# A four-layer graph stack on one core: own row and row pairs of the layer-2 heads added on GpSimd, output weights held stationary, and the row weighting of layers 1 and 3 put on GpSimd

## The chip, the core and the metric

The kernel runs on one core of a Trainium2 chip. The metric is device time in microseconds (us) of one execution, the median of a few runs. Matmuls run on TensorE (PE in the profile, its weight loads PEld), elementwise work on VectorE (DVE), ScalarE (ACT) and GpSimd (POOL); SP only starts DMAs. Everything here is float32.

## The reference

Eight batches of 2048 nodes with 64 features pass through four layers. Each layer normalizes its input, applies relu, attends over the neighbours that a sparse 0/1 matrix `adj` names, and adds the result to its input:

```python
# layer 0: softmax over neighbours of h h^T / 8, times h
# layer 1: h = x W; e = leaky(s1[n] + s2[m]); softmax over neighbours; times h; elu
# layer 2: four heads h_k = x Wh_k; per head softmax over neighbours and self of h_k h_k^T, times h_k
z   = leaky_relu(concat(heads))            # 256 features
h2  = z @ Wo.T                             # 64 features
out = layernorm(leaky_relu(softmax(h2 h2^T over neighbours and self) @ h2 + bo)) * gamma + beta
# layer 3: as layer 1, with relu at the end
for each layer: x = x + layer(relu(layernorm(x)), adj)
```

## The kernel before

The 2048 nodes are 16 **row blocks** of 128 nodes (partitions); a row holds all 8 batches, 512 numbers. Neighbours are not multiplied through a dense matrix: a setup stage turns `adj` into lists, and each block gets a number of **row slots**, 84 in all. A slot is one indirect DMA on GpSimd's queue (`gather`, L227) that brings one row for each of 128 partitions into a ring of 30 slots. The first `ROWS[i]` slots of a block hold the first neighbours of the block's own nodes, so partition p belongs to node p. The other `PACKED[i]` slots hold the remaining neighbours of all its nodes packed together; a 0/1 matrix `sel` (and its transpose `selt`) tells which node each belongs to. Per block, in the order of work:

- order of blocks: 15, 14, 13, 0, 12, 11, 10, 1, 9, 2, 8, 3, 7, 4, 6, 5
- slots of each: 3, 3, 3, 17, 3, 4, 4, 8, 4, 7, 4, 6, 4, 5, 4, 5
- of these own-node slots (`ROWS`): 2, 1, 1, 7, 1, 3, 3, 5, 3, 5, 3, 5, 2, 3, 1, 4

Every layer runs as a **pipeline** over the blocks: in step n, the last stage works on an old block and the first on a new one, and stages are issued from the last to the first. Within that program order the compiler's scheduler orders each engine's instructions by its own estimates; each engine then takes its own list strictly in order.

**Weighted sums** of layers 0, 1, 3 and of layer 2's output attention are made in `weigh_sum` (L316 to L333). For each pair of slots an elementwise engine multiplies the two gathered rows with the softmax weights (L326, a tile `wg`), and TensorE adds them up in PSUM (L331): with the identity matrix as the stationary operand for own-node slots, with `selt` for packed ones. The multiplication runs on GpSimd, except in layers 1 and 3. There `first` (L464 to L485) has ScalarE copy the weights into a small PSUM tile (`tiny`, L484), and `check` passes this copy and VectorE to `weigh_sum`.

**Layer 2's heads** are stages `take2, turn, first2, second2, third2, fourth2` (L655 to L762). `first2` forms, for head pair k = 0 and 1 in turn, the queries of the block (L685, L690), spreads them to the packed slots (L697) and has VectorE multiply and reduce query times row (`dot`, L669 and L673: one pair of instructions for the own row and each slot), then exponentials on ScalarE (L381). `second2` makes the weighted sums, for each head pair: two PSUM tiles `ys`; the block's own row, weight 1, is added with two identity matmuls (L721); then for each slot GpSimd forms `wg`, 128x1024 (L724), and two matmuls add it to `ys` (L727). VectorE divides (`yn`, L731). `third2` transposes `yn` (L741), applies the head weights (L745), bias and leaky relu. `fourth2` applies the output weights `wo_sb`: 32 small matmuls of 64 columns for each block, each with another 128x128 tile of `zt` as the stationary operand (L756), a ScalarE copy (L759), and a store to a table in memory that the next stage gathers from.

Some further lines: L255 (`ln_r`, a power on GpSimd, part of each normalization), L304 (a running sum of rows on GpSimd). The file also has a dense fallback that runs only if a list overflows; it doesn't run here.

Of the kernel before, what the change touches and what calls it, by code (L numbers as in the profile page):

```python
# [8 lines left out]
F32 = mybir.dt.float32  # L9
# [4 lines left out]
OP = mybir.AluOpType  # L14
AX = mybir.AxisListType

P = 128
# [9 lines left out]
ROWS = [7, 5, 5, 5, 3, 4, 1, 2, 3, 3, 3, 3, 1, 1, 1, 2]  # L27
# [22 lines left out]
def edge_stack(ctx: ExitStack, tc: tile.TileContext, x_in, adj, w1, w1t, a1, wh, wht, bh, wo, bo,  # L50
# [9 lines left out]
    nc = tc.nc  # L60
    N, F = x_in.shape
    D = gamma.shape[0]
    B = F // D
# [10 lines left out]
    work = ctx.enter_context(tc.tile_pool(name="work", bufs=2))  # L74

    ident = const.tile([P, P], F32, name="ident")
# [51 lines left out]
    with tc.tile_pool(name="setup", bufs=1) as sp, \  # L128
# [24 lines left out]
        for h in range(H):  # L153
            p = ps_w.tile([P, D], F32, name="p")
            nc.tensor.matmul(p, wh2[:, h].rearrange("d t c -> d (t c)"), wh2[:, h, 0, :],
                             start=True, stop=True)
# [11 lines left out]
    wo_sb = const.tile([P, 2, D], F32, name="wo")  # L168
# [33 lines left out]
    def tiny(n):  # L202

        at = spot[0] if spot[0] + n <= F else 0
        spot[0] = at + n
        return bank[0][:, at:at + n]
# [106 lines left out]
    def lhs(i, t):  # L313

        return ident if t < ROWS[i] else selt(i, t - ROWS[i])

    def weigh_sum(i, st, w, own=None, eng=nc.gpsimd):

        y = ps_y.tile([P, F], F32, name="y")
        g, n = st["g"], SLOTS[i]  # L320
        if own is not None:
            nc.tensor.matmul(y, ident, own, start=True, stop=False)
        for t0 in range(0, n, 2):
            m = min(2, n - t0)
            wg = work.tile([P, 2, F], F32, name="wg")
            eng.tensor_tensor(  # L326
                wg[:, :m].rearrange("p t (b d) -> p t b d", b=B),
                g[:, t0:t0 + m, :F].rearrange("p t (b d) -> p t b d", b=B),
                w[:, t0:t0 + m, :, None].to_broadcast([P, m, B, D]), op=OP.mult)
            for t in range(t0, t0 + m):  # L330
                nc.tensor.matmul(y, lhs(i, t), wg[:, t - t0, :], start=(t == 0 and own is None),  # L331
                                 stop=(t == n - 1))
        return y  # L333
# [63 lines left out]
        w = slots(w_all, i)  # L397
        exps(i, w, scores(i, st, st["rows"]), mba, D ** -0.5)

    def second(i, st, wp=None):  # L400
        w = slots(w_all, i)
        d, p = by_query(i, w, B)
        st["rec"] = small.tile([P, B], F32, name="rec")
        nc.vector.tensor_tensor(st["rec"], p, d, op=OP.add)
        nc.vector.reciprocal(st["rec"], st["rec"])
        st["y"] = weigh_sum(i, st, w) if wp is None else weigh_sum(i, st, wp, eng=nc.vector)
        done(i, st)

    def divide(st, dst):
# [35 lines left out]
    def additive(k, wd, *finish):  # L445
        def take(i, st):
            gather(k, i, st)

        def sums(i, st):
            w = slots(w_all, i)  # L450
            nc.scalar.activation(w, st["g"][:, :, F:], AF.Exp, scale=1.0 / TEMP)
            d, p = by_query(i, w, B)
            S = small.tile([P, B], F32, name="S")
            nc.vector.tensor_tensor(S, p, d, op=OP.add)
            nc.vector.tensor_reduce(most[:, 1, i:i + 1], S, AX.X, OP.max)
            nc.vector.tensor_reduce(least[:, 1, i:i + 1], S, AX.X, OP.min)
            lg = tiny(B)
            nc.scalar.activation(lg, S, AF.Ln)
            st["fs"] = small.tile([P, 2, B], F32, name="fs")
            z = small.tile([P, B], F32, name="z")  # L460
            nc.vector.scalar_tensor_tensor(z, lg, TEMP, f1s[:, i, :], op0=OP.mult, op1=OP.add)
            nc.scalar.copy(st["fs"][:, 0, :], f1s[:, i, :])
            leaky(st["fs"][:, 1, :], z)

        def first(i, st):
            K, T, g = ROWS[i], PACKED[i], st["g"]
            w = slots(w_all, i)
            s = slots(s_all, i)
            fs = st["fs"].rearrange("p t b -> p (t b)") if k == 4 else f1s[:, i, :]
            n = 2 * B if k == 4 else B  # L470
            pr = tiny(2 * B)
            nc.scalar.copy(pr[:, :n], fs)
            pv = by_edge(i, fs, n)
            nc.vector.tensor_tensor(s[:, :K, :], g[:, :K, F:], pr[:, None, :B].to_broadcast([P, K, B]), op=OP.add)
            nc.vector.tensor_tensor(s[:, K:, :], g[:, K:, F:], pv[:, :, :B], op=OP.add)
            leaky(s, s)
            if k == 4:
                nc.vector.tensor_tensor(s[:, :K, :], s[:, :K, :], pr[:, None, B:].to_broadcast([P, K, B]),
                                        op=OP.subtract)
                nc.vector.tensor_tensor(s[:, K:, :], s[:, K:, :], pv[:, :, B:], op=OP.subtract)  # L480
                nc.vector.tensor_scalar(s, s, 60.0, None, op0=OP.min)
            nc.scalar.activation(w, s, AF.Exp)  # L482
            wp = tiny((K + T) * B)
            nc.scalar.copy(wp, w.rearrange("p t b -> p (t b)"))  # L484
            st["wp"] = wp.rearrange("p (t b) -> p t b", b=B)  # L485

        def check(i, st):
            second(i, st, st["wp"])
            if k == 1:
                nc.vector.tensor_reduce(most[:, 0, i:i + 1], st["rec"], AX.X, OP.max)  # L490
                nc.vector.tensor_reduce(least[:, 0, i:i + 1], st["rec"], AX.X, OP.min)

        def third(i, st):
            st["att"] = work.tile([P, F], F32, name="att")
            divide(st, st["att"])
            st["xt"] = transposed(st["att"])

        def project(i, st):
            p = st["p"] = ps_q.tile([P, F], F32, name="q")
            for j in range(F // P):  # L500
                nc.tensor.matmul(p[:, j * P:(j + 1) * P], st["xt"][:, j, :], wd, start=True, stop=True)
            finish[0](i, st)

        mid = [sums] if k == 4 else []
        pipeline(take, *mid, first, both(check, xs_rows), third, project, *finish[1:])
# [145 lines left out]
    with tc.tile_pool(name="l2", bufs=2) as l2p, \  # L651
# [54 lines left out]
        def second2(i, st):  # L706
            g, n = st["g"], SLOTS[i]
            w = st["w"]
            d, p = by_query(i, w.rearrange("p t b h -> p t (b h)"), B * H)
            rec = st["rec"] = small.tile([P, B, H], F32, name="rec2")  # L710
            rf = rec.rearrange("p b h -> p (b h)")
            nc.vector.scalar_tensor_tensor(rf, p, 1.0, d, op0=OP.add, op1=OP.add)
            nc.vector.tensor_reduce(most[:, 2, i:i + 1], rf, AX.X, OP.max)
            nc.vector.reciprocal(rf, rf)
            st["yn"] = []
            for k in range(2):
                hs = slice(2 * k, 2 * k + 2)
                ys = [ps_y.tile([P, 4, 2, D], F32, name="y") for _ in range(2)]
                xb = heads(st["rows"])[:, :, None, :].to_broadcast([P, B, 2, D])
                for j in range(2):  # L720
                    nc.tensor.matmul(ys[j], ident, xb[:, 4 * j:4 * j + 4], start=True, stop=False)  # L721
                for t in range(n):
                    wg = work.tile([P, B, 2, D], F32, name="wg")
                    nc.gpsimd.tensor_tensor(wg, heads(g[:, t, :F])[:, :, None, :].to_broadcast([P, B, 2, D]),  # L724
                                            w[:, t, :, hs, None].to_broadcast([P, B, 2, D]), op=OP.mult)
                    for j in range(2):
                        nc.tensor.matmul(ys[j], lhs(i, t), wg[:, 4 * j:4 * j + 4], start=False,  # L727
                                         stop=(t == n - 1))
                for j in range(2):
                    yn = l2p.tile([P, 4, 2, D], F32, name="yn", bufs=4)  # L730
                    nc.vector.tensor_tensor(yn, ys[j], rec[:, 4 * j:4 * j + 4, hs, None].to_broadcast([P, 4, 2, D]),  # L731
                                            op=OP.mult)
                    st["yn"].append(yn.rearrange("p b h d -> p (b h d)"))
            done(i, st)
# [15 lines left out]
                st["zt"].append(zt)  # L750

        def fourth2(i, st):
            p = ps_m.tile([P, F], F32, name="m")
            for b in range(B):
                for k in range(2):
                    nc.tensor.matmul(p[:, b * D:(b + 1) * D], st["zt"][2 * k + b // 4][:, b % 4, :],  # L756
                                     wo_sb[:, k, :], start=(k == 0), stop=(k == 1))
            h2 = work.tile([P, F + B], F32, name="xh", bufs=3)
            nc.scalar.copy(h2[:, :F], p)  # L759
            store_rows(3, i, h2, False)  # L760

        pipeline(take2, turn, first2, second2, third2, fourth2)  # L762
# [1 line left out]
    with psum_pools()[0] as ps_q, psum_pools()[1] as ps_t, tc.tile_pool(name="rows2", bufs=2) as rp:  # L764
# [66 lines left out]
        p = ps_m.tile([P, F], F32, name="m")  # L831
# [516 lines left out]
```

## Time and profile before

| | us |
|---|---|
| median of 3 runs | 2215.48 (2214.14 to 2217.83) |
| the profiled execution: its time | 2214.14 |
| its span, first to last instruction | 2212.4 |
| busy PE / DVE / POOL / ACT | 1535.5 / 1404.1 / 1108.3 / 615.7 |
| mean granted TensorE clock | 0.821 |

The stages follow one another in the trace, with the gathers of a stage waiting for the table that the stage before stored:

| stage | window, us | PE busy | DVE busy | POOL busy |
|---|---|---|---|---|
| layer 1 | 475 to 710 | 152.5 | 126.4 | 109.6 |
| layer 2, heads | 710 to 1624 | 756.5 | 558.7 | 397.0 |
| layer 3 | 1985 to 2212 | 155.4 | 100.1 | 80.3 |

In a group line, the name left of the arrow is the tile written, the ones right of it the tiles read; then shapes, the number of instructions, busy us, mean ns of one, and the idle time just before. A float32 matmul stands in the trace as two MATMUL records, so 672 records of L727 are 336 matmuls. Matmuls are pipelined, so their mean is longer than their share of busy time. "issue" in a chain or wait is time in which the profile shows no releaser.

### The profile page before, as it was taken

How to read it: one execution, taken by the hardware profiler on the slowest of the kernel's cores; microseconds unless marked ns; L12 is line 12 of the kernel's file. 1: busy time of each engine (PE TensorE's matmuls, PEld its weight loads, DVE VectorE, ACT ScalarE, POOL GpSimd, SP SyncE). 2: the span in 40 equal slices, each digit the busy share in tenths (PEclk: the TensorE clock that was granted, in tenths of full speed). 3: DMA queues.
4: the chain of work that ended last, by engine and by line, in shares of the span. 5: the costliest groups of instructions: out<-in, count | busy, mean ns of one | idle time of the engine just before them, and what ended most of it. 6: DMA issues, size and time to landing. Idle time of an engine off the chain costs nothing.

```text
span 2212.4 us, 17548 instructions
## 1 busy us (share of the span) xinstructions
PE 1535.5 (69%) x5020; PEld 819.4 (37%) x5020; DVE 1404.1 (63%) x2891; ACT 615.7 (28%) x1714; POOL 1108.3 (50%) x857
## 2 busy tenths in 40 slices
PE   0226766656684598968968888899867666653887
PEld 0113433433342254424533434454433233332544
DVE  5798699734675479507664747676547677751455
ACT  3412223221343030202301212222222444442233
POOL 5736666555533540583516352434447766445340
PEclk9957676767788798999979889999987777756789
DMA  5543445346543300020101110000044432126461
GB/s 171 161 147 105 144 142 171 102 131 179 173 131 121 107 25 19 5 76 29 34 29 43 29 38 15 5 10 5 5 148 142 124 119 81 43 72 178 125 187 54
DMA packets 77726, 200.75 MB, mean 91 GB/s; under 512 B 13827, under 2 KB 13827, under 8 KB 75574
## 3 DMA queue, kind: packets, MB, share of 16 engines
q0 software_dynamic: 33920, 110.93, 17.4%
q1 hardware_dynamic: 43702, 88.63, 11.9%
q8 instruction: 41, 0.67, 0.1%
q14 instruction: 63, 0.52, 0.1%
HBM read 161.61 MB, written 37.90 MB: 90 GB/s over the span
## 4 chain that ended last, share of the span: by engine, by line
PE 32%; POOL 21%; DVE 17%; issue 17%; ACT 7%; another core or an unknown queue 3%; DMA 2%; SPq 0%; POOLq 0%; DVEq 0%; ACTq 0%
POOL wg L724 8%; PE y L331 8%; PE y L727 7%; POOL g L227 6%; POOL ln_r L255 4%; POOL wg L326 3%; PE q L697 3%; ACT xh L260 2%; PE m L745 2%; PE m L756 2%; DVE prod L669 2%; PE m L343 1%; PE m L290 1%; PE q L268 1%
## 5 line engine op out<-in xcount | busy, mean ns | idle before, releaser
L227 POOL DMA_INDIRECT g<-table,idx x420 | 414.5, 987 | 296.7 <-issue 126.7
L724 POOL TENSOR_TENSOR wg<-g,s 128x1024 f32<-128x1024 f32 x168 | 320.0, 1913 | 471.8 <-ACT s L381 349.2
L331 PE MATMUL y<-wg,ident 128*128 128x512 f32 x392 | 266.1, 818 | 98.8 <-POOL wg L326 71.0
L669 DVE TENSOR_TENSOR prod<-q,g 128x1024 f32<-128x1024 f32 x168 | 200.5, 1216 | 28.3 <-PE q L697 23.8
L727 PE MATMUL y<-wg,ident 128*128 128x512 f32 x392 | 193.1, 617 | 33.4 <-POOL wg L724 33.4
L255 POOL TENSOR_TENSOR ln_r<-ln_q,mhalf 128x8 f32<-128x8 f32 x80 | 140.4, 1757 | 149.0 <-DVE ln_q L253 111.2
L326 POOL TENSOR_TENSOR wg<-g,w 128x1024 f32<-128x1024 f32 (+1 forms) x92 | 162.5, 1776 | 77.8 <-issue 29.8
L673 DVE TENSOR_REDUCE s<-prod 128x16 f32<-128x1024 f32 x168 | 199.4, 1208 | 0.4
L260 ACT ACTIVATE xh<-ln_xc,ln_r 128x64 f32<-128x64 f32 x512 | 135.4, 336 | 187.3 <-POOL ln_r L255 187.3
L731 DVE TENSOR_TENSOR yn<-y,rec 128x512 f32<-128x512 f32 x64 | 43.5, 689 | 202.8 <-PE y L727 202.6
L331 PEld LDWEIGHTS y<-wg,ident 128*128 128x128 f32 x392 | 92.0, 259 | 211.3 <-POOL wg L326 104.2
L331 PE MATMUL y<-wg,selt 128*128 128x512 f32 x280 | 156.5, 681 | 18.3 <-POOL wg L326 15.2
L697 PE MATMUL q<-qn,sel 128*128 128x512 f32 x280 | 145.0, 649 | 34.8 <-DVE prod L669 15.5
L727 PE MATMUL y<-wg,selt 128*128 128x512 f32 x280 | 138.8, 618 | 28.1 <-POOL wg L724 28.0
L690 ACT COPY qn<-q 128x512 f32<-128x512 f32 x64 | 34.3, 589 | 373.4 <-PE q L685 358.1
L326 DVE TENSOR_TENSOR wg<-g,tiny 128x1024 f32<-128x1024 f32 (+1 forms) x92 | 101.6, 1114 | 26.0 <-PE y L331 21.4
L727 PEld LDWEIGHTS y<-wg,ident 128*128 128x128 f32 x392 | 70.1, 195 | 118.1 <-POOL wg L724 60.9
L373 PE MATMUL q<-rows,sel 128*128 128x512 f32 x140 | 95.4, 802 | 20.0 <-DVE prod L375 8.2
L331 PEld LDWEIGHTS y<-wg,selt 128*128 128x128 f32 x280 | 60.9, 225 | 106.5 <-issue 72.1
L343 PE MATMUL m<-w,selt 128*128 128x8 f32 x350 | 61.8, 288 | 54.9 <-ACT w L482 26.2
L697 PEld LDWEIGHTS q<-qn,sel 128*128 128x128 f32 x280 | 55.6, 207 | 106.5 <-issue 79.2
L343 PEld LDWEIGHTS m<-w,selt 128*128 128x128 f32 x350 | 62.9, 248 | 84.8 <-ACT w L482 36.0
(212 smaller groups left out, 2685.6 us busy)
## 6 DMA issues: line engine op xcount, KB each, us to landing
a<-in_adj_dram SPq DMA_DIRECT2D x16, 1024.0 KB
table<-xh SPq DMA_DIRECT2D x48, 256.0 KB
rows<-table SPq DMA_DIRECT2D x48, 256.0 KB
xs<-x SPq DMA_DIRECT2D x48, 256.0 KB
x<-xs SPq DMA_DIRECT2D x48, 256.0 KB
table<-xh SPq DMA_DIRECT2D x32, 260.0 KB
x<-in_x_dram SPq DMA_DIRECT2D x32, 256.0 KB
g<-table,idx POOLq DMA_INDIRECT x420
```

Of the source, the lines that this page charges most:

```text
L227: nc.gpsimd.indirect_dma_start(out=ring[:, at + t, :cols], out_offset=None, in_=table[k][:, :], in_offset=bass.IndirectOffsetOnAxis(ap=idx ...
L255: nc.gpsimd.tensor_tensor(st["rstd"], q, mhalf, op=OP.pow)
L260: nc.scalar.activation(dst[:, b * D:(b + 1) * D], st["xc"][:, b * D:(b + 1) * D], func, scale=st["rstd"][:, b:b + 1])
L326: eng.tensor_tensor(wg[:, :m].rearrange("p t (b d) -> p t b d", b=B), g[:, t0:t0 + m, :F].rearrange("p t (b d) -> p t b d", b=B), w[:, t0: ...
L331: nc.tensor.matmul(y, lhs(i, t), wg[:, t - t0, :], start=(t == 0 and own is None), stop=(t == n - 1))
L343: nc.tensor.matmul(p[:, :cols], selt(i, t), w[:, K + t, :], start=(t == 0), stop=(t == T - 1))
L373: nc.tensor.matmul(qe, sel(i, t - K), q, start=True, stop=True)
L669: nc.vector.tensor_tensor(pr.rearrange("p (b o) h d -> p b o h d", o=2), q, rows.rearrange("p (b o d) -> p b o d", o=2, d=D)[:, :, :, None ...
L673: nc.vector.tensor_reduce(dst, pr, AX.X, OP.add)
L697: nc.tensor.matmul(qe[:, b0:b0 + 4], sel(i, t), qn[:, b0:b0 + 4], start=True, stop=True)
L724: nc.gpsimd.tensor_tensor(wg, heads(g[:, t, :F])[:, :, None, :].to_broadcast([P, B, 2, D]), w[:, t, :, hs, None].to_broadcast([P, B, 2, D] ...
L727: nc.tensor.matmul(ys[j], lhs(i, t), wg[:, 4 * j:4 * j + 4], start=False, stop=(t == n - 1))
```

## The change

Three edits go together.

1. `weigh_sum` has no engine argument any more; layers 1 and 3 multiply on GpSimd with the weights where `Exp` left them, and the copy to PSUM is gone.
2. In `second2` the identity matmuls for the own row are gone: GpSimd adds the own row to the first slot's weighted row. From the second slot on, two own-node slots at a time are added up on GpSimd, and only the sum goes to TensorE. The weighted rows have a pool of three buffers of their own (`wh`) instead of two.
3. `fourth2` holds `wo_sb` (64 columns) stationary and streams `zt` in four matmuls of 512 columns; the result stands transposed, so ScalarE copies it to SBUF, four TensorE transposes turn it, and the last copy puts the columns in order.

```diff
-    def weigh_sum(i, st, w, own=None, eng=nc.gpsimd):
+    def weigh_sum(i, st, w, own=None):
...
-            eng.tensor_tensor(
+            nc.gpsimd.tensor_tensor(
                 wg[:, :m].rearrange("p t (b d) -> p t b d", b=B),
...
-        st["y"] = weigh_sum(i, st, w) if wp is None else weigh_sum(i, st, wp, eng=nc.vector)
+        st["y"] = weigh_sum(i, st, w)
...
             nc.scalar.activation(w, s, AF.Exp)
-            wp = tiny((K + T) * B)
-            nc.scalar.copy(wp, w.rearrange("p t b -> p (t b)"))
-            st["wp"] = wp.rearrange("p (t b) -> p t b", b=B)
 
         def check(i, st):
-            second(i, st, st["wp"])
+            second(i, st)
...
                 xb = heads(st["rows"])[:, :, None, :].to_broadcast([P, B, 2, D])
-                for j in range(2):
-                    nc.tensor.matmul(ys[j], ident, xb[:, 4 * j:4 * j + 4], start=True, stop=False)
-                for t in range(n):
-                    wg = work.tile([P, B, 2, D], F32, name="wg")
+
+                def weighted(t):
+                    wg = l2p.tile([P, B, 2, D], F32, name="wh", bufs=3)
                     nc.gpsimd.tensor_tensor(wg, heads(g[:, t, :F])[:, :, None, :].to_broadcast([P, B, 2, D]),
                                             w[:, t, :, hs, None].to_broadcast([P, B, 2, D]), op=OP.mult)
+                    return wg
+
+                t = 0
+                while t < n:
+                    wg, first = weighted(t), t == 0
+                    if first:
+                        nc.gpsimd.tensor_tensor(wg, wg, xb, op=OP.add)
+                    elif t + 1 < ROWS[i]:
+                        t += 1
+                        nc.gpsimd.tensor_tensor(wg, wg, weighted(t), op=OP.add)
                     for j in range(2):
-                        nc.tensor.matmul(ys[j], lhs(i, t), wg[:, 4 * j:4 * j + 4], start=False,
-                                         stop=(t == n - 1))
+                        nc.tensor.matmul(ys[j], lhs(i, t), wg[:, 4 * j:4 * j + 4], start=first, stop=(t == n - 1))
+                    t += 1
...
         def fourth2(i, st):
             p = ps_m.tile([P, F], F32, name="m")
-            for b in range(B):
+            for j in range(2):
                 for k in range(2):
-                    nc.tensor.matmul(p[:, b * D:(b + 1) * D], st["zt"][2 * k + b // 4][:, b % 4, :],
-                                     wo_sb[:, k, :], start=(k == 0), stop=(k == 1))
+                    nc.tensor.matmul(p[j * D:(j + 1) * D, :], wo_sb[:, k, :],
+                                     st["zt"][2 * k + j].rearrange("p b n -> p (b n)"), start=(k == 0), stop=(k == 1))
+            ht = work.tile([P, F], F32, name="att")
+            nc.scalar.copy(ht, p)
+            p = ps_m.tile([P, F], F32, name="m")
+            for b in range(4):
+                nc.tensor.transpose(p[:, b * P:(b + 1) * P], ht[:, b * P:(b + 1) * P], ident)
             h2 = work.tile([P, F + B], F32, name="xh", bufs=3)
-            nc.scalar.copy(h2[:, :F], p)
+            nc.scalar.copy(h2[:, :F].rearrange("p (j b d) -> p b j d", j=2, d=D),
+                           p.rearrange("p (b j d) -> p b j d", j=2, d=D))
             store_rows(3, i, h2, False)
```

In layer 2 this makes 32 additions of the own row (16 blocks, 2 head pairs) and 30 of pairs: of slots 1, 2, ... below `ROWS[i]`, 15 pairs over all blocks, each for 2 head pairs.

More of the change, by code (lines that the diff above doesn't have):

```diff
@@ L398, in first0, with second @@
         exps(i, w, scores(i, st, st["rows"]), mba, D ** -0.5)
-    def second(i, st, wp=None):
+    def second(i, st):
         w = slots(w_all, i)
```

## The prediction, on record before the changed kernel ran

> **What bounds the kernel now.** I read the busy table by stage first, then groups by line with shapes kept apart, then the waits in layer 2, then GpSimd's timeline, and for each stage the chain that ended last. In the stage rows the columns are length, then busy us (instructions) of PE, PE loads, DVE, ACT, POOL, then granted clock:
>
> ```profile
> 475.00:710.00 235.00, 152.48 (x522) 89.23 (x522) 126.36 (x298) 77.82 (x241) 109.59 (x103) 0.76 0.51 155
> 710.00:1624.00 914.00, 756.46 (x2668) 385.11 (x2668) 558.69 (x621) 183.40 (x371) 396.98 (x247) 0.92 0.10 31
> 1985.00:2212.00 227.00, 155.40 (x581) 95.73 (x581) 100.07 (x318) 68.84 (x143) 80.25 (x85) 0.76 0.45 134
> ```
>
> In layer 2 (second row) TensorE is busy 83%, GpSimd 43%: it looks like a TensorE stage with GpSimd to spare. The waits say otherwise (engine, who it waited for, us in total, times, longest):
>
> ```profile
> POOL wg L724 <- ACT s L381: 349.2, 17, 49.7
> DVE yn L731 <- PE y L727: 202.6, 45, 53.3
> POOL wg L724 <- PE y L727: 121.4, 73, 11.0
> ```
>
> GpSimd is idle because it has nothing to weight until VectorE has all scores of the next block and ScalarE their exponentials (first line). Then VectorE stands at `yn` until the sums are made (second). The two take turns, and in the second head pair GpSimd sets the pace:
>
> ```profile
> 1202.66 1.92 POOL L724 TENSOR_TENSOR wg<-g,s 128x1024 f32<-128x1024 f32 x1
> 1204.85 0.99 POOL L227 DMA_INDIRECT g<-table,idx  x1 [0.27 <-POOL wg L724]
> 1205.86 1.92 POOL L724 TENSOR_TENSOR wg<-g,s 128x1024 f32<-128x1024 f32 x1
> 1208.04 0.99 POOL L227 DMA_INDIRECT g<-table,idx  x1 [0.27 <-POOL wg L724]
> ```
>
> A gather lies between weightings, so a slot costs 3.19 us (1.92 + 0.27 + 0.99), where TensorE needs 1.98. Over 745 to 1624 the chain gives GpSimd's weighting 19.1% and gathers 5.1%, the sums L727 18.3%, the own-row matmuls L721 only 1.9%, L756 5.4%.
>
> **What the Trainium skill says.** "GPSIMD Engine Reference", 3.1 Elementwise: a float32 `tensor_tensor` add of 2048 elements takes 4497 ns on GpSimd, half as fast as VectorE. So 1024 take about 2.25 us, an estimate from that page. The running sum below (1.286 us for 512) agrees; the weighting, whose weights repeat over 64 columns, is cheaper, 1.913 us for 1024. "TensorE: Matmul & The Clock Gate", Architectural detail, says that GpSimd takes instructions strictly in order; the trace agrees: `ln_r` waits behind gathers in layer 1. The same page, Part 1, says that idle stretches of TensorE lower its clock; the trace grants 0.92 in layer 2, 0.76 in layers 1 and 3, so TensorE relieved of work may get a lower clock. I price that at nothing, at most 5 us.
>
> The rows that I price with:
>
> ```profile
> L724 POOL TENSOR_TENSOR wg<-g,s 128x1024 f32<-128x1024 f32 x168 | 320.0, 1913 | 471.8 <-ACT s L381 349.2 <-PE y L727 121.4 <-ACT att L743 0.2
> L326 POOL TENSOR_TENSOR wg<-g,w 128x1024 f32<-128x1024 f32 x76 | 146.1, 1930 | 70.3 <-issue 29.8 <-ACT w L381 22.2 <-PE y L331 17.9
> L326 DVE TENSOR_TENSOR wg<-g,tiny 128x1024 f32<-128x1024 f32 x76 | 91.1, 1206 | 21.6 <-PE y L331 17.1 <-issue 3.3 <-DVE wg L326 0.5
> L721 PE MATMUL y<-rows,ident 128*128 128x512 f32 x128 | 66.8, 637 | 8.3 <-DVE yn L731 8.3
> L304 POOL TENSOR_TENSOR acc<-acc,xh 128x512 f32<-128x512 f32 x45 | 57.9, 1286 | 38.2 <-ACT xh L260 35.2 <-ACT tiny L472 2.7
> ```
>
> **Layers 1 and 3.** VectorE loses 46 weightings a layer (38 of 1024, 8 of 512 elements: 51 us), ScalarE 16 copies of 0.18 us. GpSimd gains 38 x 1.92 + 8 x 1.04 = 81 us, plus 0.15 us between instructions, 7 us. In the built order they stand between the gathers, so gathers now queue behind weightings that wait for exponentials.
>
> Layer 1: GpSimd starts at 472.5 and must do 84 gathers x 1.25 us (0.95 and a gap of 0.30) = 105, 13 `ln_r` x 1.85 = 24, and 88: 217 us, to 690. The last weighting ended at 683.6 before: +6. GpSimd also waited 13.2 us for the first `ln_r` (523.1); it still stands there, behind block 0's gathers: +12. Small waits: +2. The tail after the last weighting (20 us) stays. **+20 us**, since GpSimd becomes the bound.
>
> Layer 3: 105 + 88 = 193 us from 1991.4, to 2185, against 2193.6 before. But weights come late: it reaches block 15's 4 us early (first weighting 2006.9), and block 0's at about 2053, when they were ready at 2066 before and block 0's gathers now end some 7 us later behind two weightings and that wait: 18 us. With 2 for the rest: 2185 + 24 - 2194 = **+15 us**.
>
> Between them these waits are the least certain term: from +5 (VectorE's 51 us shorten the chain, and GpSimd catches up) to +30 each.
>
> **Layer 2, TensorE's part.** Removed: 64 own-row matmuls (66.8 us) and 60 of 336 of L727 (331.9 / 336 = 0.99 each: 59 us). `fourth2` had 75.9 / 16 = 4.7 us a block; now four matmuls at 0.99 and four transposes (L741: 43.2 / 64 = 0.68) make 4.6: even. It adds a ScalarE copy of 0.59 a block, between the matmuls and the transposes. Behind the transposes on TensorE's list stand the next queries and `third2`; the built order puts four query matmuls into that gap, so the copy is hidden but in the last block, where copy and transposes are late: +1. TensorE falls from 756 to about 630 us. It was 83% busy but not alone on the path.
>
> **Layer 2, GpSimd's part.** 62 additions of 1024. Bounds: 1.91 (as L724) to 2.41 (L304 doubled, less one start of 0.16). I take 2.3: 143 us, 540 of 914 in all. Single instructions of these rows took longer (L304 up to 2.13 us), so the upper end is not firm.
>
> A block with n slots and p pairs now holds GpSimd 2n x 1.91 + 2(1 + p) x 2.3, plus 1.27 for each gather between (waits for TensorE gone: third buffer, fewer matmuls). Set against the stretch from its first to its last weighting before:
>
> - block 1 (n 8, p 2): 30.6 + 13.8 + 8.9 = 53.3 against 44.2: +9
> - blocks 2 and 3: 48.1 against 38.6, 41.7 against 29.0: +10, +13
> - 9, 8, 4, 5 (p 1): +3, +2, +3, +2; 11 and 10: 29.6 against 24.5 and 21.6: +5, +8
> - 15, 14: +3, +1; 7: -3; 6: -2 (VectorE bounds it); 13 and 12: 0, hidden behind VectorE's 87 us of block 0's scores and behind waits that go
> - block 0 (n 17, p 3): the first head pair's additions run while VectorE still works on its packed scores; that pair then ends at about 936 instead of 946; the second takes 32.5 + 9.2 + 19 = 61 instead of 53: -2
>
> Sum +52; the drain makes +1 more.
>
> Against that, VectorE's built order differs: more products of the next block stand ahead of the second `yn`, where VectorE had waited. Each that moves is 2.42 us (1.216 + 1.208) off the tail after `yn`: 7 beside block 10, some 7 beside block 0, 4, 3 and 1 beside blocks 1, 2 and 3, less 1 beside block 11: 21 x 2.42 = 51, of which I count all, and 6 of small waits for TensorE (VectorE's waits on L697 were 23.8 in all). 53 - 57 = **-4 us**: layer 2 stays about where it is. TensorE gives up 126 us, and almost nothing of it shows.
>
> **Sum.** 20 + 15 - 4 = +31. The profiled execution took 2214.1 (span 2212.4 and 1.7 around it): 2245. The median is 1.3 above it: 2246.
>
> **The rivals.**
>
> - **A, the forecast:** as above, 2246 (2222 to 2270 by the bounds of the waits and the additions). 0.55.
> - **B, all GpSimd time is path in layer 2:** the reordered products wait for queries that TensorE makes late, since its own list stands at sums that wait for additions. Then only some 12 of the 57 come back: 2246 + 45 = 2291. For it: waits on `yn` of up to 53 us behind GpSimd's pace. 0.20.
> - **C, TensorE decides in layer 2, faster:** for it, 83% busy and 121 us in which GpSimd waited for L727. Its share of the chain is 879 us x (1.9% + 18.3% x 60/336) = 46 us, with half of the 23.8 us of waits on L697 58 us off; additions hide under exponentials and TensorE. 2246 + 4 - 58 = 2192. It decides once layer 2 gives more than layers 1 and 3 cost, 35 us. Against it: 349 us of GpSimd's idle time lie before the exponentials, where no addition can go. 0.20.
> - **D, layers 1 and 3 cost nothing:** VectorE's 51 us a layer come off the chain (wg has 6.0% and 5.0% of it) and balance GpSimd's: 2246 - 33 = 2213. 0.05.
>
> Range: A, most of B and C: 2196 to 2292. Within 0.2% (4.4 us, about what a measurement of this kernel can tell from no change) lies D: 0.05; faster C, 0.20; slower A and B, 0.75.
>
> **What would show it.** Right: in layers 1 and 3 GpSimd is busy over 75% and about 20 and 15 us longer; additions near 2.3 us; layer 2 at 890 to 930 us with TensorE near 630; waits of `yn` still near 200. Wrong: layer 2 below 880 (C) or above 940 (B); additions at 1.9, which would take 25 us of GpSimd's time away; gathers in layer 1 never late (D).

## The result, and the profile after

| kernel | median us | range, runs |
|---|---|---|
| before | 2216.19 | 2214.14 to 2217.83, 4 |
| changed | 2243.8 | 2232.45 to 2247.47, 4 |

The ratio is 1.0116 (95% interval 1.0077 to 1.0155). The profiled execution took 2241.16 us, its span is 2239.3.

Stage by stage, each counted from its first gather to the first gather of the next (layer 3 to the end of the span):

| stage | before | changed | difference | forecast |
|---|---|---|---|---|
| up to layer 1 | 472.5 | 473.7 | +1.2 | |
| layer 1 | 231.4 | 248.0 | +16.6 | +20 |
| layer 2, heads | 923.7 | 913.1 | -10.6 | -4 |
| layer 2, output attention | 363.8 | 365.5 | +1.7 | |
| layer 3 | 221.0 | 238.9 | +17.9 | +15 |

The busy table by stage of the changed kernel (columns as in the prediction's first fence):

```profile
475.00:710.00 235.00, 151.97 (x498) 82.65 (x498) 88.76 (x245) 68.59 (x212) 185.34 (x144) 0.78 0.48 143
710.00:1624.00 914.00, 668.14 (x2110) 306.35 (x2110) 563.08 (x626) 194.55 (x396) 546.19 (x315) 0.86 0.11 34
1985.00:2239.00 254.00, 166.84 (x594) 99.09 (x593) 62.23 (x275) 66.09 (x137) 165.14 (x133) 0.76 0.43 122
```

The rows use the same windows as the table before; the changed kernel's layer 2 really runs from 721.7 to 1634.9 us, where TensorE is busy 676 us. In layer 1 GpSimd is now busy 185.3 of 235 us, 79%, where it had 109.6. In layer 2 it rose from 397 to 546, and TensorE fell from 756 to 668, not to 630, at a mean granted clock of 0.86 instead of 0.92.

The waits between 725 and 1620 us:

```profile
POOL wh L720 <- ACT s L381: 297.1, 16, 52.6
DVE yn L738 <- PE y L734: 134.9, 41, 28.3
PEld y L734 <- POOL wh L732: 65.8, 24, 7.5
```

GpSimd still waits for exponentials, 297 us. VectorE's wait at the division fell from 202.6 to 134.9. The third line is new: TensorE now waits for an addition on GpSimd ahead of a sum.

The groups on GpSimd:

```profile
L720 POOL TENSOR_TENSOR wh<-g,s 128x1024 f32<-128x1024 f32 x168 | 319.2, 1915 | 318.2 <-ACT s L381 297.1 <-PE y L734 19.1
L729 POOL TENSOR_TENSOR wh<-wh,rows 128x1024 f32<-128x1024 f32 x32 | 75.3, 2354 | 1.4
L732 POOL TENSOR_TENSOR wh<-wh 128x1024 f32<-128x1024 f32 x30 | 70.4, 2347 | 1.9
```

The 62 additions take 2.35 us each, 146 us (forecast 2.3). The page "GPSIMD Engine Reference" of the Trainium skill, 3.1 Elementwise, led to 2.25, a little low. GpSimd's wait for TensorE (last figure of the first row) is 19.1 us where it was 121.4.

A second head pair on GpSimd's timeline (start, length, instruction, idle time before):

```profile
1206.89 1.92 POOL L720 TENSOR_TENSOR wh<-g,s 128x1024 f32<-128x1024 f32 x1
1208.97 0.99 POOL L227 DMA_INDIRECT g<-table,idx  x1 [0.16 <-issue]
1209.97 2.36 POOL L732 TENSOR_TENSOR wh<-wh 128x1024 f32<-128x1024 f32 x1
```

An addition takes its place in the queue like a weighting, and a gather still lies between most of them.

TensorE's matmuls of the sums, with the own-node slots (identity stationary) and the packed ones (`selt`) apart, before and after:

```profile
L727 PE MATMUL y<-wg,ident 128*128 128x512 f32 x392 | 193.1, 617 | 33.4 <-POOL wg L724 33.4
L727 PE MATMUL y<-wg,selt 128*128 128x512 f32 x280 | 138.8, 618 | 28.1 <-POOL wg L724 28.0
L734 PE MATMUL y<-wh,ident 128*128 128x512 f32 x272 | 171.0, 757 | 113.5 <-POOL wh L732 51.1 <-POOL wh L729 42.7 <-DVE yn L738 16.1
L734 PE MATMUL y<-wh,selt 128*128 128x512 f32 x280 | 138.6, 628 | 13.2 <-POOL wh L720 13.2
```

A packed sum takes 0.99 us as before (138.6 / 140). An own-node sum, which now often waits for an addition, takes 171.0 / 136 = 1.26 us, where it took 193.1 / 196 = 0.99. The timeline shows how, with two matmuls (four records) in each line:

```profile
1205.77 3.78 PE L734 MATMUL y<-wh,ident 128*128 128x512 f32 x4 [7.29 <-POOL wh L732]
1212.38 1.98 PE L734 MATMUL y<-wh,ident 128*128 128x512 f32 x4
```

After 7.29 us of standing for an addition the pair takes 3.78 us, at a granted clock of 0.50 in that stretch; the pair that follows other matmuls takes 1.98 us at 1.00.

### The profile page after: what moved, and what is told of

The parts are those of the page before. It is cut to its first block, busy times and chain, and to the rows that moved or that the text cites. A ratio compares the mean times of both kernels' runs of the same rounds, so it can differ in the third digit from the quotient of the medians.

```text
span 2239.3 us, 16459 instructions
## 1 busy us (share of the span) xinstructions
PE 1464.2 (65%) x4452; PEld 740.3 (33%) x4452; DVE 1334.9 (60%) x2799; ACT 613.8 (27%) x1696; POOL 1415.5 (63%) x1011
## 3 DMA queue, kind: packets, MB, share of 16 engines
q1 hardware_dynamic: 43702, 88.63, 11.8%
## 4 chain that ended last, share of the span: by engine, by line
POOL 25%; issue 18%; PE 14%; DVE 4%; ACT 3%; another core or an unknown queue 2%; DMA 1%; ACTq 0%; POOLq 0%; SPq 0%; DVEq 0%
POOL wh L720 8%; POOL g L227 7%; PE y L331 4%; PE y L734 4%; POOL wg L326 3%; POOL wh L732 3%; POOL wh L729 3%; POOL ln_r L255 1%; DVE prod L666 1%; PE m L752 1%; PE q L694 1%; PE m L343 1%; DVE s L670 1%; PE m L290 1%
## 5 line engine op out<-in xcount | busy, mean ns | idle before, releaser
L720 POOL TENSOR_TENSOR wh<-g,s 128x1024 f32<-128x1024 f32 x168 | 319.2, 1915 | 318.2 <-ACT s L381 297.1
L326 POOL TENSOR_TENSOR wg<-g,w 128x1024 f32<-128x1024 f32 (+1 forms) x184 | 321.1, 1757 | 125.3 <-issue 33.3
L331 PE MATMUL y<-wg,ident 128*128 128x512 f32 x392 | 282.7, 857 | 166.5 <-POOL wg L326 138.8
L734 PE MATMUL y<-wh,ident 128*128 128x512 f32 x272 | 171.0, 757 | 113.5 <-POOL wh L732 51.1
L666 DVE TENSOR_TENSOR prod<-q,g 128x1024 f32<-128x1024 f32 x168 | 200.6, 1215 | 29.5 <-PE q L694 26.3
L331 PEld LDWEIGHTS y<-wg,ident 128*128 128x128 f32 x392 | 92.5, 263 | 285.0 <-POOL wg L326 187.7
L331 PE MATMUL y<-wg,selt 128*128 128x512 f32 x280 | 169.2, 724 | 24.2 <-POOL wg L326 24.2
L734 PE MATMUL y<-wh,selt 128*128 128x512 f32 x280 | 138.6, 628 | 13.2 <-POOL wh L720 13.2
L738 DVE TENSOR_TENSOR yn<-y,rec 128x512 f32<-128x512 f32 x64 | 43.2, 688 | 135.2 <-PE y L734 134.9
L734 PEld LDWEIGHTS y<-wh,ident 128*128 128x128 f32 x272 | 56.3, 230 | 186.7 <-POOL wh L732 65.8
L410 DVE TENSOR_TENSOR att<-y,rec 128x512 f32<-128x512 f32 x32 | 22.1, 691 | 138.5 <-PE y L331 138.5
L390 DVE TENSOR_TENSOR zt<-m,att 128x512 f32<-128x512 f32 x64 | 44.0, 688 | 87.4 <-ACT m L387 84.5
```

Source lines behind the costliest of these rows:

```text
L326: nc.gpsimd.tensor_tensor(wg[:, :m].rearrange("p t (b d) -> p t b d", b=B), g[:, t0:t0 + m, :F].rearrange("p t (b d) -> p t b d", b=B), w[ ...
L666: nc.vector.tensor_tensor(pr.rearrange("p (b o) h d -> p b o h d", o=2), q, rows.rearrange("p (b o d) -> p b o d", o=2, d=D)[:, :, :, None ...
```

## Experiments

The comparisons ran on two chips: on one the kernel before takes 2212 to 2215 us, like the 2216 of the first pair, on the other 2163 to 2164. I call them the first and the other chip. Each ratio is against runs on the same chip. For layer 2 I also give a stretch that doesn't depend on how the layer starts: from block 15's last division (the first block) to block 5's (the last), in the profile. It is 837.7 us for the kernel before in its first profile and 835.4 in its second, 823.2 and 816.3 for the changed kernel, so a difference of less than some 7 us between two profiles says little. It hardly depends on the chip: with layer 2 as before it is 836.6 on the other (edit 1 alone, below).

### One edit at a time

**Edit 1 alone**, GpSimd's weightings in layers 1 and 3, layer 2 as before.

```diff
-            eng.tensor_tensor(
+            nc.gpsimd.tensor_tensor(
...
-            second(i, st, st["wp"])
+            second(i, st)
```

> The first edit alone: weighting of layers 1 and 3 on GpSimd, layer 2 as in the kernel before. My theory (GpSimd's queue becomes the bound of both layers): layer 1, from its first gather to layer 2's first, 246 to 250 us (231.4 before, 248.0 changed), layer 3 to the end 236 to 241 us (221.0 before), layer 2 as before within 4 us; total 2244 to 2254, ratio 1.014 to 1.017. Rival (the loss is of the three edits together, for instance by a lower clock of TensorE in layer 2): ratio 1.000 to 1.008.

Measured: 2235.86 us against 2164.22, ratio 1.0325 (1.0305 to 1.0345), more than either theory. Layer 1 takes 247.9 us and layer 3 235.9, as in the changed kernel, but on this chip the kernels that leave these layers alone take 208.6 to 210.0 and 197.2 to 203.6. The edit costs 72 us in all here, about 38 a layer against the kernels with 209 and 197.

**Edit 2 alone**, `second2` of the changed kernel in the kernel before.

> The second edit alone: own row and pairs on GpSimd in layer 2, the rest as before. My theory (layer 2 has no engine alone on its path; GpSimd's additions cancel what TensorE and the reordering give): layer 2 between 909 and 922 us (923.7 before, 913.1 changed), ratio 0.993 to 1.000. Rival C (TensorE decides): layer 2 at 880 or below, ratio under 0.982. Rival B (all additions are path): layer 2 at 950 or above, ratio over 1.012.

Measured: 2171.82 us, ratio 1.0035 (1.0022 to 1.0047), just above the range of my theory and far from both rivals. The stretch is 839.0 us.

**Edit 3 alone**, `fourth2` of the changed kernel.

> The third edit alone: output weights stationary, then transposes. My theory (4.7 against 4.6 us of TensorE a block, a copy more that is hidden): layer 2 within 5 us of 923.7, ratio 0.998 to 1.002. Rival (the output step is the part of layer 2's gain, 32 weight loads of 128 columns less a block): layer 2 at 905 to 915, ratio 0.992 to 0.996.

Measured: 2129.01 us, ratio 0.9844 (0.9827 to 0.9861), a gain beyond the rival's. The stretch is 805.9 us, 30 to 32 shorter. TensorE's timeline at a block where the granted clock is 1.00 in both, kernel before first (the output matmuls, 16 with two records each, where the description of the kernel says 32; then the next block's queries):

```profile
1336.71 3.79 PE L756 MATMUL m<-wo,zt 128*128 128x64 f32 x32 [0.68 <-ACT xt L664]
1340.43 0.49 PE L685 MATMUL q<-q,xt 64*128 64x128 f32 x4
```

```profile
1274.54 1.94 PE L757 MATMUL m<-zt,wo 128*64 128x512 f32 x8 [0.68 <-ACT xt L664]
1276.42 0.49 PE L685 MATMUL q<-q,xt 64*128 64x128 f32 x2
```

The queries, for which VectorE's next products wait, start 1.88 us after the output step's start instead of 3.72; the transposes come behind them. They follow at once in 6 of the 16 blocks; elsewhere other matmuls stand between. In the group rows of the changed kernel L764 has 41.5 us and L770 11.8, together 3.3 us a block, against 75.9 / 16 = 4.7 for L756. Block by block, 14 of the 30 us lie between block 11's and block 1's last division, where this edit also changes VectorE's order (next part); the rest is spread over the other blocks.

**The third buffer alone**, a size hidden in edit 2.

```diff
-                    wg = work.tile([P, B, 2, D], F32, name="wg")
+                    wg = l2p.tile([P, B, 2, D], F32, name="wh", bufs=3)
```

> Kernel before with one thing changed: three buffers of their own for layer 2's weighted rows. In the trace before, GpSimd waited 121.4 us for TensorE to free one of two buffers. My theory: that wait is mostly beside other waits, since sums go no faster than TensorE; layer 2 falls by 2 to 10 us, ratio 0.995 to 0.999. Rival (layer 2's gain in the changed kernel is the third buffer, not fewer matmuls): layer 2 falls by 20 us or more, ratio under 0.991, and the additions then cost the difference. Second rival: nothing changes, 0.999 to 1.001.

Measured: 2146.33 us, ratio 0.9914 (0.9898 to 0.9929), 18 us off, where I had expected 2 to 11. The stretch is 819.0 us, and GpSimd's waits for TensorE fell from 121.4 to 66.1 us. With the same buffer, edit 2 alone takes 20 us more of stretch: its additions cost more than its removed matmuls and its new order bring, though the order has 17 more products ahead of second divisions than here.

### The two kernels again, and the order by itself

> The kernel before, unchanged, to see its stages on the chip of this comparison. Theory (the stalls of all engines at the start of layers 1, 2 and 3 belong to the first profile's chip): where the kernel before takes about 2164 us, layer 1 takes 208 to 213 us and layer 3 196 to 204 us, as in the kernels with only layer 2 edited, and the waits of 10 to 20 us without a releaser at the start of these layers are gone; layer 2's heads take 910 to 920 us. Where it takes about 2215 us they are there again, and layers 1 and 3 take 231 and 221 us. Rival (the two layers take what they take on any chip, and the difference of 51 us lies in layers 0 and 2): layer 1 at 225 us or more whatever the time.

Measured: 2215.41 us (this chip's kernel before: 2212.44). Layer 1 232.6 us and layer 3 220.8, as in the first profile; a kernel with only layer 2 edited, run beside it, has 231.2 and 220.9. So the same code in these layers takes 23 us less in each on the other chip. TensorE's timeline in layer 1, here and then on the other chip (the kernel with edit 3 alone):

```profile
489.12 1.88 PE L331 MATMUL y<-wg,selt 128*128 128x512 f32 x4
494.43 2.08 PE L501 MATMUL q<-wd,xt 128*128 128x128 f32 x8 [3.43 <-issue]
501.57 1.11 PE L268 MATMUL q<-ident,att 128*128 128x128 f32 x4 [5.07 <-issue]
```

```profile
487.60 1.88 PE L331 MATMUL y<-wg,selt 128*128 128x512 f32 x4
489.32 1.05 PE L501 MATMUL q<-wd,xt 128*128 128x128 f32 x8
490.27 0.66 PE L268 MATMUL q<-ident,att 128*128 128x128 f32 x4
```

On the first chip TensorE stands for nothing that the profile shows. In layer 3 such stands of over 2.5 us add up to 19 to 24 us, most or all of the difference; in layer 1 only to 4 to 11, and VectorE and ScalarE have some there too. On the other chip TensorE has none in either layer. What causes them was not tried, and layer 1's 23 us are not accounted for in full. The changed kernel has such stands on the first chip too, 7 to 15 us a layer, but its layer 1 is no longer there than that of edit 1 alone on the other chip.

> The changed kernel, unchanged, beside the kernel before on the chip of this comparison. Theory (with GpSimd's queue as the bound, layers 1 and 3 take 248 and 236 to 239 us on any chip, and what differs is only how long the kernel before takes there): where the kernel before takes about 2164 us, the ratio is 1.025 to 1.032, where it takes about 2215 us, 1.010 to 1.015. Rival (the ratio is a property of the change): 1.008 to 1.016 in both cases.

Measured: 2236.12 us, ratio 1.0118 (1.007 to 1.0166), as the theory has it for a chip of 2212 us, where the rival gives the same. Layer 1 247.1 us (+14.5), layer 2's heads 905.6 (-16.7), layer 3 240.5 (+19.7). The changed kernel as a whole wasn't run on the other chip. The product of the ratios measured there for edit 1 (1.0325) and edits 2 and 3 (0.9977, below) is 1.030, an estimate.

**The order alone.** The compiler's scheduler reorders VectorE's list whenever an edit moves its estimates. In the list built for edit 3 alone, 7 more products of block 1 stand ahead of block 10's second division than before; in the trace of edit 2 alone the same 7 do, so that edits 2 and 3 together move them only once. This kernel makes just that change, in the kernel before:

```diff
+        ahead, begun = {10: 3}, {}
...
+            if i in ahead:
+                j = ORDER[ORDER.index(i) + 1]
+                begun[j] = parts2(j, held2[j])
+                for _ in range(ahead[i]):
+                    next(begun[j])
             g, n = st["g"], SLOTS[i]
```

(`parts2` is `first2` with a stop behind each product.)

> The kernel before with one change of order: the program issues the own-row product and two slots of block 1's first head pair ahead of block 10's weighted sums. In the built order 9 products (7 and 2) instead of 2 then stand ahead of block 10's division into the output, as in the kernel with the output edit alone; all else is as before. Theory (more than half of what the output edit alone gave in layer 2 is this order: 7 products of 2.42 us come off the stretch in which VectorE works alone): 17 to 20 us off, ratio 0.990 to 0.993, all of it between block 10's and block 1's last division. Rival (the output edit gave its time because TensorE and ScalarE wait less in the output step itself): 0.998 to 1.001.

Measured: 2200.62 us, ratio 0.9956 (0.9937 to 0.9976). Layer 2's heads take 908.5 us against 922.3; 13.6 us of it lie between block 11's and block 1's last division (114.2 against 127.9), and nothing elsewhere. So the theory was right on the place and a little high on the size: 13.6 / 7 = 1.9 us a product, not 2.42. VectorE's timeline beside block 10, before and then with the order changed:

```profile
1096.84 0.69 DVE L390 TENSOR_TENSOR zt<-m,att 128x512 f32<-128x512 f32 x1 [1.55 <-ACT m L387]
1100.77 0.69 DVE L390 TENSOR_TENSOR zt<-m,att 128x512 f32<-128x512 f32 x1 [3.24 <-ACT m L387]
...
1117.50 0.69 DVE L731 TENSOR_TENSOR yn<-y,rec 128x512 f32<-128x512 f32 x1 [9.01 <-PE y L727]
...
1120.10 1.22 DVE L669 TENSOR_TENSOR prod<-q,rows 128x1024 f32<-128x1024 f32 x1 [1.05 <-ACT qn L690]
```

```profile
1098.16 1.22 DVE L672 TENSOR_TENSOR prod<-q,rows 128x1024 f32<-128x1024 f32 x1 [0.30 <-ACT qn L695]
1099.30 1.21 DVE L672 TENSOR_TENSOR prod<-q,g 128x1024 f32<-128x1024 f32 x1
...
1121.36 0.69 DVE L748 TENSOR_TENSOR yn<-y,rec 128x512 f32<-128x512 f32 x1 [3.93 <-PE y L744]
```

Before, VectorE does little from 1097 to 1120: it stands between the output maxima and 9.01 us at the division, and only then begins block 1's products. Reordered, the same products fill these gaps, and the division is 3.9 us later (1121.36 against 1117.50). That delay is about what the seven products lose of their 2.42 us each.

### What the additions cost, and what is left without them

**Buffer and output step, no additions.**

> The third buffer for layer 2's weighted rows and the new output step, without any addition on GpSimd and with layers 1 and 3 as before. Theory (the buffer shortens GpSimd's stretches, the output edit VectorE's, so both gains stand side by side): 45 to 53 us off, ratio 0.975 to 0.979. Rival (both shorten the same wait, VectorE's at the division): no more than the larger of the two, ratio 0.982 to 0.986.

Measured: 2159.07 us against 2212.44, ratio 0.9755 (0.9722 to 0.9789). The gains add up (53 us, against 18 and 35 alone); the stretch is 779.8 us, 56 below the kernel before.

**The own row's additions only**, on top of that.

```diff
-                    elif t + 1 < ROWS[i]:
-                        t += 1
-                        nc.gpsimd.tensor_tensor(wg, wg, weighted(t), op=OP.add)
```

(against the changed kernel's `second2`, so that the pairs' additions are gone)

> Buffer and output step, and of the additions only the own row's (32 of 62), with layers 1 and 3 as before. VectorE's built order is that of the kernel with buffer and output step alone but for 3 products beside block 11, so this is the price of the 32 additions, 75 us of GpSimd's time, against 64 matmuls of TensorE, 67 us. Theory (GpSimd sets the pace in the second head pair, so about half of the additions lie on the path, and the matmuls removed give little): 20 to 35 us longer than that kernel, ratio 0.985 to 0.991. Rival (GpSimd's waits for the exponentials, near 300 us, take the additions in): within 5 us, 0.973 to 0.978.

Measured: 2165.18 us against 2163.08, ratio 1.0008 (0.9998 to 1.0018), worse than both theories. The stretch is 832.0 us, 52 more than without them. That is the net price of 32 additions, 75 us of GpSimd's time, and of 64 matmuls less on TensorE; the two weren't tried apart, so whether the removed matmuls gave anything is not shown. The sums that remain kept TensorE busy for 342 us instead of 321.

**Edits 2 and 3 together**, layers 1 and 3 as before.

> The edits of layer 2 together (additions on GpSimd with their third buffer, and the new output step), with layers 1 and 3 as before. Theory (layer 2 gains by the buffer, by the output step and by VectorE's order, and gives back most of it to the additions): layer 2's heads 14 to 20 us shorter than in the kernel before, ratio 0.990 to 0.994, and 35 to 42 us longer than with buffer and output step alone (0.9755). Rival, the prediction as it stood (the additions and the order cancel, layer 2 within 4 us of the kernel before): ratio 0.997 to 1.000.

Measured: 2157.88 us, ratio 0.9977 (0.9968 to 0.9985), inside the rival's range; my theory, taken from the 16.7 us of the other chip, missed. The stretch is 825.7 us, 6 less than with the own row only: 30 more additions, 70 us of GpSimd's time, come with 60 matmuls less and some 14 more products moved ahead of a second division, and these about cancel. I haven't separated them.

**Buffer, output step, and the order written out.**

```diff
+        ahead, begun = {0: 6, 11: 5, 10: 5, 1: 8, 9: 5, 2: 6, 8: 5, 3: 6, 7: 5, 4: 5, 6: 5}, {}
```

> Buffer and output step without additions, as in the kernel of ratio 0.9755, and with an order written into the program: for each block from block 0 on, 4 to 8 score products of the block after it are issued ahead of its weighted sums. In the built order as many products stand ahead of each second division as in the changed kernel, or up to 4 more, 28 more in all than in the kernel of ratio 0.9755. Theory (each product moved into VectorE's wait for the sums is worth 1.9 us, as block 10's seven were): 25 to 50 us off that kernel, ratio 0.953 to 0.964. Rival (only block 10's wait was long enough, elsewhere the products run later but the sums do too): 0.972 to 0.978.

Measured: 2068.23 us against 2163.08, ratio 0.958 (0.9563 to 0.9598): the fastest of all. The stretch is 741.3 us, 38.5 below the kernel without the written order, 1.4 us for each of 28 products. So the theory was right, at a little less for each product; beside block 12 two fewer stand ahead than in the changed kernel, not as many.

**Half of the weightings of layers 1 and 3 on GpSimd**, on top of that.

```diff
+            eng, v = (nc.gpsimd, w) if wp is None or t0 % 4 else (nc.vector, wp)
             eng.tensor_tensor(
```

> As the kernel with the order written out, and in layers 1 and 3 every second pair of slots (21 of 46) is weighted on GpSimd, the others on VectorE as before. GpSimd's queue work in layer 1 is then 129 + 21 x 2.07 = 172 us, below the layer's length. Theory (the changed kernel loses in layers 1 and 3 because the whole queue, 217 us, becomes longer than the layer): layers 1 and 3 within 6 us each of what they take with all weightings on VectorE. Rival (each weighting on GpSimd is later on the path, whatever the queue's length): 21/46 of the changed kernel's loss, 7 to 9 us in each layer where the kernel before takes 2212 us, 17 in each where it takes 2164 us.

Measured: 2123.37 us, ratio 0.9822 (0.9802 to 0.9843). Layer 1 takes 229.4 us against 208.9 with all weightings on VectorE, layer 3 227.0 against 197.5. So my theory fell and the rival's size is nearer: the loss comes long before the queue is full. GpSimd's timeline in layer 1 shows where, with the weightings on VectorE (the kernel of 0.958) and then on GpSimd (edit 1 alone):

```profile
530.36 0.96 POOL L227 DMA_INDIRECT g<-table,idx  x1 [0.30 <-issue]
531.63 0.95 POOL L227 DMA_INDIRECT g<-table,idx  x1 [0.31 <-issue]
```

```profile
534.94 1.91 POOL L326 TENSOR_TENSOR wg<-g,w 128x1024 f32<-128x1024 f32 x1
537.02 0.99 POOL L227 DMA_INDIRECT g<-table,idx  x1 [0.17 <-issue]
538.03 1.91 POOL L326 TENSOR_TENSOR wg<-g,w 128x1024 f32<-128x1024 f32 x1
540.10 0.99 POOL L227 DMA_INDIRECT g<-table,idx  x1 [0.16 <-issue]
```

A gather every 1.25 us becomes a gather every 3.1. On this chip the 84th gather of layer 1 starts 131.6 us after the first with no weighting ahead of it, 153.4 with 15, 178.6 with 35; the layer lasts 77, 76 and 69 us beyond that. So the layer's length goes with the gathers' stream, and weightings put into it push the later gathers back. A kernel with the same weightings behind the gathers wasn't run, so that this alone makes the loss is argued, not shown. On the first chip the kernel before, with no weighting in the stream, has this gather only at 154.9, and the changed kernel at 178.9: there the edit moves it by 24 us, here by 47.

## Why the prediction was right, and where its steps were not

The time, its sign and the order of size of its parts came out as forecast (+24 to +28 us against +31), but it was luck in part: errors cancel, in layers 1 and 3 between the mechanism and the chip, in layer 2 between terms much larger than their sum. Two of the signs named for "right" didn't come: TensorE near 630 us (668) and waits of `yn` near 200 (134.9).

- **Layer 1 (+20; +16.6 and +14.5).** The signs named came: GpSimd busy 79%, gathers late. The step "since GpSimd becomes the bound", 217 us of queue work that just passes the old end, is not the mechanism: with 172 us of queue work the layer still lost 20.5. The timelines point to the place of the weightings ahead of gathers. The +12 for the first `ln_r` didn't come: it started at 518.3 without a wait. The size fits only because the kernel before is 23 us longer on this chip, its gathers late already; on the other chip the same edit costs 38.
- **Layer 3 (+15; +17.9 and +19.7).** The late weights at block 0 took 4.7 us, not 18; waits of 8.0 and 6.5 us near the end took their place. Here too half of the weightings cost more than in proportion, 29.5 us of 38; why two engines in turn do so badly there stays open.
- **Layer 2, GpSimd's part.** Additions at 2.35 us: right. Reordered products: right in kind, and the order by itself is shown to give time, but 1.4 to 1.9 us each, not "all" of 2.42; and the trace has 16 more ahead of second divisions, not 21, among other things because beside block 12 there are 3 fewer. The third buffer stood inside the blocks' sums as "waits for TensorE gone"; it is worth 18 us alone. The own row's additions cost 52 us, net of the matmuls removed, where I had +52 for all 62 with the buffer's gain taken off.
- **Layer 2, TensorE's part.** The step that failed is "even". It priced the four output matmuls at the 0.99 us of sums with 128 stationary columns; with 64 they took 41.5 / 64 = 0.65 on average, and 1.94 / 4 = 0.49 at a granted clock of 1.00. So the output step costs 3.3 us a block, not 4.6, and its matmuls stand ahead of the queries. Edit 3 alone gave 30 us of stretch, of which the order explains 13.6; that the earlier queries gave the rest is likely but not shown. The other step is the clock, priced at nothing: own-node sums that wait for additions run at a lower clock, 1.26 us each instead of 0.99, 37 us over 136 of them. The two errors go against each other, and with rises of 1 to 6 us in other matmuls TensorE stands at 668 and not 630 us.
- **Rivals.** C fell: layer 2 stayed far above 880 us, and where 64 matmuls went for 32 additions the stretch became 52 us longer. B fell: additions lie on the path, but the buffer, the output step and the order give their time back. D fell in all comparisons.

So where did the gain go? The buffer (-18), the output step with its 7 products (-30) and the rest of the order (about 10 more products at 1.4 to 1.9 us, an estimate of 14 to 19 beyond that) are in the changed kernel, 62 to 67 us if they add up. Layer 2 shows 11 to 19 of it, so the additions, net of the matmuls removed, return some 43 to 56, an estimate by difference. Layers 1 and 3 lose 34 us on top.

## What to carry to other kernels

An engine that is idle half of the time may still have no room: here GpSimd's idle time lay before the exponentials, while its busy stretches, between gathers, set the pace. Before work goes onto a queue that issues transfers, count how many transfers stand behind it, not only how full the queue is. Matmuls taken from an engine that then stands between the others are not worth their full time: the ones left may run at a lower clock. Split a change into its parts, the small ones (a buffer, the built order) too: here a third buffer gave 18 us and 7 moved products 13.6, while additions in place of matmuls lost time.

## What the runs showed of the hardware

- The same code of layers 1 and 3 takes 209 and 197 us on the other chip and 231 and 221 on the first. On the first, TensorE stands 3 to 20 us at a time with no releaser in the profile at the start of the layers, while gathers keep the DMA engines busy (55% from 488 to 525 us, 70% from 2014 to 2035 in the kernel before). That accounts for most or all of layer 3's difference and for less than half of layer 1's; what it stands for wasn't tried.
- TensorE's granted clock falls where it has stood: in the changed kernel a pair of sums after 7.29 us of waiting ran at 0.50 and took 3.78 us, a pair without a wait ran at 1.00 and took 1.98. The mean over layer 2 was 0.86 and 0.89 in the two profiles of the changed kernel, 0.92 before, and 0.96 in the fastest kernel (busy 707 of 818 us, 86%). It doesn't follow the busy share alone: two kernels busy 76 and 77% had 0.86 (edit 2 alone) and 0.92 (buffer, output step and own row). The page "TensorE: Matmul & The Clock Gate" of the Trainium skill, Part 1, says that an idle stretch lowers the clock; the runs agree, and show what it does to the matmuls that remain.
- At a granted clock of 1.00, four output matmuls with 64 stationary columns and 512 streamed took 1.94 us, where 16 with 128 stationary and 64 streamed took 3.79. Two sums with 128 stationary and 512 streamed took 1.98, so half as many stationary columns took about half the time for each matmul.
